# Two score blocks behind one product, and chain products two slots apart, in an attention kernel on one core

## The chip, the cores and the metric

The kernel runs on one core of a Trainium2 chip. The time is device microseconds (us) of one execution of the whole program. The engines are named as in the profile: PE (TensorE, matmuls), PEld (its weight loads, which run beside the matmuls), DVE (VectorE), ACT (ScalarE), POOL (GpSimd) and SP (SyncE, which here only issues DMAs). Each engine works through its own queue in order and waits on semaphores for the others.

## The reference

One layer of graph attention, for 128 graphs of 128 nodes, 768 features and 12 heads of 64, all in float32:

```python
h = jnp.maximum(_layernorm(x, axis=-1), 0.0)
q = _split_heads(h @ Wq + bq)          # likewise k, v
scores = jnp.einsum('bhqd,bhkd->bhqk', q, k) / jnp.sqrt(64)
scores = scores + beta * adj_e
scores = jnp.where(adj_e > 0, scores, -9e15)
probs = jax.nn.softmax(scores, axis=-1)
out = jnp.einsum('bhqk,bhkd->bhqd', probs, v)
x = x + out                            # heads put side by side again
```

## The kernel before

**Groups and slices.** Four graphs make a group; there are 32 groups, numbered 0 to 31. Of each group three matrix products are made, called slices: `qk0` (Q and K of the first six heads), `v` (V), and `qk1` (Q and K of the other heads). Group 0 is done in a plain way while the weights are prepared. From group 1 on each slice is a 3x3 block product done with a fast scheme of 15 block products instead of 27 (`PRODUCTS`, with sums of activations `SUMS_A` on one side and prepared weights on the other). One block product is again split into 7 zones, and is 14 matmuls in the program and 28 in the trace, where a float32 matmul stands twice (L547). The loop over the groups is written out in full; nothing is a loop on the chip.

**Slots.** The order of the 15 products in a slice is a table: `ZORDER` for `qk0` and `v`, `QORDER` for `qk1`, `LORDER` for the last group's `qk1`. A place in this order is called a slot, 0 to 14, and "slot 2 of V" is the third product of a V slice. All other work is hung on slots by hand with `then(slot, function, ...)`: it is put into the engines' queues after that slot's product and before the reading of its result, or, with `(slot, "post")`, after that reading. `later(f, n)` puts f off by n slots.

**Chains.** Each product belongs to one of four chains, a to d. A chain's products add up in one pair of PSUM banks, so the next product of a chain must wait until the running sum has been read. The reading goes to one or two of the six output blocks (r, j) of the slice: the first use of an output block copies it (in Q/K slices three instructions on ACT, L565 and L567 twice; in V slices first L561 on DVE and then L562 on ACT), and each later use adds on DVE (L571). There are four pairs of banks; chains, score blocks and the sums with V take and give them in turn (`take`, `give`).

**Homes and decoding.** An output block lies in one of eight tiles (`home`; one of them is a part of `sbig`). When its last product has been added, `decode` (L589 to L592, four instructions; in V slices L600 to L604) makes the final values in place, one slot later or as `LAG` says. It runs on POOL, except that in `qk1` the block that product 13 completes is decoded on DVE.

**Scores.** A score block (`scores`, L626) takes Q and K of one output column j for both r, 32 matmuls in the trace with 64 rows and 64 columns of the array (64\*64 in the profile), where products and the sums with V use 128 rows (128\*64). One slot later the mask is applied on DVE (L634), which also gives back the PSUM banks, and behind that the exponential on ACT (L636). Three blocks of `qk1` are placed in the next group's `qk0` slice, and the three of `qk0` in the group's own `v` slice. Weighing with V (L683), normalising (L654, L666), adding (L708) and storing follow at later slots.

**Other work on slots.** `norm` (L446) applies the layer norm of the next group on ACT, two instructions at a time; `to_hT` (L459) transposes on DVE; `sum_acts` (L464) makes the `SUMS_A` on DVE; `inner` (L469 to L471) adds on POOL; `row_stats` (L417 to L419) works on ACT out of a row loaded by DMA, for the group after the next. Prepared weights (`T`) are read from DRAM through a ring of 5 buffers (L335 by the loads of `T_qk` and `T_v`), one load being issued on SP after each product that used one; the products at the places listed in `RESIDENT` keep theirs in SBUF.

The order in which the engines get their instructions is exactly the order of these calls. The lines of the changed part in the kernel before:

```python
ZORDER = (1, 0, 3, 5, 2, 7, 10, 6, 11, 13, 4, 9, 14, 8, 12)
ORDER = {"qk0": ZORDER, "v": ZORDER, "qk1": QORDER}
RESIDENT = (3, 8, 12, 16, 20, 25, 29, 33, 35, 38, 41)
...
engine = nc.vector if sl == "qk1" and (n == 13 or last and n in (11, 12, 14)) else nc.gpsimd
...
then(3, scores, G - 1, 1, 2)          # qk0
then(5, scores, G - 1, 1, 0)
then((6, "post"), scores, G - 1, 1, 1)
...
then(0, scores, G, 0, 2)              # v
then(2, scores, G, 0, 1)
then(7, scores, G, 0, 0)
```

Of the kernel before, what the change touches and what calls it, by code (L numbers as in the profile page):

```python
# [108 lines left out]
ZORDER = (1, 0, 3, 5, 2, 7, 10, 6, 11, 13, 4, 9, 14, 8, 12)  # L109
QORDER = (4, 0, 1, 8, 2, 3, 5, 6, 7, 10, 9, 11, 13, 12, 14)  # L110
LORDER = (1, 4, 0, 8, 5, 2, 10, 3, 6, 7, 13, 9, 11, 12, 14)
ORDER = {"qk0": ZORDER, "v": ZORDER, "qk1": QORDER}
RING = 5
RESIDENT = (3, 8, 12, 16, 20, 25, 29, 33, 35, 38, 41)

# [10 lines left out]
def direct(ctx, tc, x, adj, wq, bq, wk, bk, wv, bv, beta, out, bad):  # L126
# [10 lines left out]
    nc = tc.nc  # L137
# [121 lines left out]

    sequence = [(sl, n) for sl in ("qk0", "v", "qk1") for n in ORDER[sl]]  # L260
    resident = {key: const.tile([P, 7, P], F32, name=f"res_{key[0]}_{key[1]}") for key in (sequence[at] for at in RESIDENT)}
# [59 lines left out]
        return steps  # L321

    def order_of(G, sl):
        return LORDER if G == NG - 1 and sl == "qk1" else ORDER[sl]

    ring = [(G, sl, n) for G in range(1, NG) for sl in ("qk0", "v", "qk1") for n in order_of(G, sl)
            if (sl, n) not in resident]
    nt = [0]

    def load_T():  # L330
        if nt[0] < len(ring):
            G, sl, n = ring[nt[0]]
            nt[0] += 1
            t = tz[G, sl, n] = work.tile([P, 7, P], F32, tag="T", name=f"T_{G}_{sl}_{n}", bufs=RING)
            nc.sync.dma_start(t, kept[sl, n])  # L335
# [125 lines left out]
    def sum_acts(G, name):  # L461
        _, a, b, sign = [row for row in SUMS_A if row[0] == name][0]
        t = full[G, name] = block(SPOT.index(name))
        nc.vector.tensor_tensor(t, full[G, a], full[G, b], ALU.add if sign > 0 else ALU.subtract)  # L464
# [33 lines left out]
    def later(f, slots=1):  # L498
        while len(deferred) < slots:
            deferred.append([])  # L500
        deferred[slots - 1].append(f)
# [6 lines left out]
    def turn():  # L508

        while between and next(between[0], None) is None:  # L510
            between.popleft()
# [4 lines left out]
    def home_qk(G, sl, r, j, zones=False):  # L516
        t = home_of[G, sl, r, j] = homes.popleft()
        return t if zones else t[:, 0:4].rearrange("p (i g) n -> p i (g n)", i=2)
# [12 lines left out]
    def product_z(G, sl, n):  # L531

        an, bn, chain, uses = PRODUCTS[n]
        mine = [i for i in order_of(G, sl) if PRODUCTS[i][2] == chain]
        first = n == mine[0]
        if first:
            banks[chain] = take()
        p = banks[chain].rearrange("p i (z w) -> p (i z) w", w=P)
        a = full[G, an]
        streamed = (sl, n) not in resident  # L540
        b = tz.pop((G, sl, n)) if streamed else resident[sl, n]
        for at, z in enumerate(ZONES):
            lhs, rhs = a[:, LEFT[z]], b[:, RIGHT[z]]
            if sl != "v":
                lhs, rhs = rhs, lhs
            for q in range(0, P, HD):
                nc.tensor.matmul(p[q:q + HD, at, :], lhs[:, q:q + HD], rhs, start=(first and at % 4 == 0),  # L547
                                 stop=True, skip_group_check=True)
            turn()
        if streamed:  # L550
            load_T()
        yield
        for (r, j), sign in uses:
            key = (G, sl, r, j)
            op = ALU.add if sign > 0 else ALU.subtract
            if key not in qk:
                left[key] = sum(k == (r, j) for q in PRODUCTS for k, _ in q[3])
                t = qk[key] = home_qk(*key, zones=True)
                if sl == "v":
                    bias = bv_b[:, j * 2 * P:(j + 1) * 2 * P].rearrange("p (i n) -> p i n", i=2)  # L560
                    nc.vector.tensor_tensor(t[:, 5:7], bias, p[:, 5:7], op)  # L561
                    nc.scalar.activation(t[:, 0:5], p[:, 0:5], AF.Copy, scale=float(sign))  # L562
                else:
                    oc = j + 3 * int(sl[2])
                    nc.scalar.activation(t[:, 0:5], p[:, 0:5], AF.Copy, scale=float(sign))  # L565
                    for at, of in ((5, 0), (6, 2)):
                        nc.scalar.activation(t[:, at], p[:, at], AF.Identity, bias=bqk[:, of, oc:oc + 1],  # L567
                                             scale=float(sign))
            else:
                t = qk[key]  # L570
                nc.vector.tensor_tensor(t, t, p[:, 0:7], op)  # L571
            left[key] -= 1
            if not left[key]:
                last = order_of(G, sl) is LORDER
                engine = nc.vector if sl == "qk1" and (n == 13 or last and n in (11, 12, 14)) else nc.gpsimd
                later(lambda r=r, j=j, engine=engine: decode(G, sl, r, j, engine), 1 if last else LAG.get((sl, n), 1))
        if n == mine[-1]:
            give(banks.pop(chain))
        yield
# [236 lines left out]
    def slice_z(G, sl, todo):  # L816
        run([product_z(G, sl, n) for n in order_of(G, sl)], todo)
# [163 lines left out]
    def then(at, f, *args):  # L981
        todo.setdefault(at, []).append(lambda: f(*args))

    def bias(G, *at):
        def go():
            if G not in steps:
                steps[G] = bias_steps(G)
            next(steps[G], None)
        for n in at:
            then(n, go)  # L990

    def attention(G, u, at, behind=5):
        for n, j in at:
            then(n - 3, load_xo, G, 3 * u + j)
            then((n, "post"), attend, G, 3 * u + j, behind)
# [6 lines left out]
    def turn_act(G, slots, behind=0):  # L1002
        for at, name in slots:
            then(at, to_hT, G, int(name[1]), int(name[2]))
            if behind is not None:
                then(at + behind, inner, G, name)

    def sums_at(G, slots):
        for at, name in slots:
            then(at, sum_acts, G, name)  # L1010
# [57 lines left out]
    for G in range(1, NG):  # L1068
        more = G + 1 < NG
        todo.clear()  # L1070
        then(3, scores, G - 1, 1, 2)
        then(5, scores, G - 1, 1, 0)
        then((6, "post"), scores, G - 1, 1, 1)
        attention(G - 1, 1, ((7, 2), (10, 0), (12, 1)))
        sums_at(G, ((0, "S7"), (1, "S0"), (4, "S5"), (7, "S14"), (9, "S11")))
        if G == 1:
            todo[0].insert(0, lambda: sum_acts(1, "S6"))
        if more:
            for g in range(2):
                for h in range(2):  # L1080
                    then((2 * g + h, "post"), norm, G + 1, g, 2 * h, 2 * h + 2)
            turn_act(G + 1, ((8, "A01"), (9, "A00"), (11, "A02")), None)
            then((12, "post"), load_x, G + 1, 1)
            if G + 2 < NG:
                then((7, "post"), row_stats, G + 2, 0)
                then((9, "post"), load_row, G + 2, 1)
        slice_z(G, "qk0", todo)

        todo.clear()
        then(0, scores, G, 0, 2)  # L1090
        then(2, scores, G, 0, 1)
        then(7, scores, G, 0, 0)
        if more:
            then((11, "post"), add_raw, G + 1)
            for n, at in enumerate((3, 4, 7, 8)):
                then((at, "post"), norm, G + 1, 2 + n // 2, n % 2 * 2, n % 2 * 2 + 2)
            turn_act(G + 1, ((10, "A11"),), 1)
            for at, name in ((4, "A01"), (5, "A00"), (6, "A02")):
                then(at, inner, G + 1, name)
            if G + 2 < NG:  # L1100
                for g, at in ((1, 1), (2, 5), (3, 10)):
                    then((at, "post"), row_stats, G + 2, g)
                    if g < 3:
                        then((at + 1, "post"), load_row, G + 2, g + 1)
        slice_z(G, "v", todo)

        todo.clear()
        if not more:
            break
        attention(G, 0, ((3, 2), (9, 1)))  # L1110
        attention(G, 0, ((12, 0),), 6)
        turn_act(G + 1, ((1, "A10"), (4, "A12")), 1)
        sums_at(G + 1, ((6, "S1"), (7, "S9"), (8, "S2"), (11, "S6"), (13, "S10")))
        bias(G + 1, 0, 2, 4)
        if G + 2 < NG:
            then(5, row_moments, G + 2, 6, 9)
            then((6, "post"), load_x, G + 2, 0)
        if G + 3 < NG:
            then((10, "post"), load_row, G + 3, 0)
        slice_z(G, "qk1", todo)  # L1120
# [158 lines left out]
```

## Time and profile before

| | |
|---|---|
| median of 3 runs | 2707.47 us (2703.18 to 2716.2) |
| profiled execution | 2712.82 us, its span 2711.0 us |
| PE busy | 2674.2 us, 99% of the span |
| PEld busy | 2568.3 us, 95% |
| DVE busy | 2188.4 us, 81% |
| POOL busy | 2096.0 us, 77% |
| ACT busy | 1762.5 us, 65% |
| DMA | 721.73 MB, mean 266 GB/s; the data queue's packets fill 86.4% of the 16 engines' time |

The profile is of one execution; its own time lies 0.2% above the median of the runs. A row of the timeline gives the start in us from the span's start, the length in us, engine, line of the kernel, operation, output tile and input tiles, shape and number of equal instructions in a row; in brackets stands the idle time before and what ended it. Matmuls overlap each other in the array, so the length of a group of matmuls reaches into the next; the pace of PE is read from the differences of the starts. A row of waits gives who waited for whom, then the us in total, the number of times, and the longest.

### The profile page before, as it was taken

The numbers are of one execution on the slowest core, as the hardware profiler recorded it, in microseconds if no ns is written. First come the engines' busy times: TensorE is split into PE (matmuls) and PEld (weight loads), VectorE is DVE, ScalarE is ACT, GpSimd is POOL, SyncE is SP. The second block draws the span as 40 slices with busy tenths as digits, with TensorE's granted clock in tenths as the row PEclk, the third lists the DMA queues.
The fourth block names the chain that finished last, engine by engine and source line by source line (L and its number), as shares of the span: only waits on it lengthen the run. The fifth ranks groups of instructions, "written<-read, shape, count | busy, mean of one in ns | idle before, by whom it ended". The sixth has DMA issues, their size and how long they took to land.

```text
span 2711.0 us, 121562 instructions
## 1 busy us (share of the span) xinstructions
PE 2674.2 (99%) x52029; PEld 2568.3 (95%) x52029; DVE 2188.4 (81%) x2705; ACT 1762.5 (65%) x4612; POOL 2096.0 (77%) x3034
## 2 busy tenths in 40 slices
PE   8999999999999999999999999999999999999997
PEld 7799999999999999999999999999999999999997
DVE  6878888788888788888788878788887888877885
ACT  2476666677666677666767666776666776667653
POOL 4867878777878877888778787778787778887783
PEclk9999999999999999999999999999999999999999
DMA  8789889899889898889899889898898988888875
GB/s 229 262 260 278 274 271 274 259 281 276 271 264 281 260 287 272 271 278 277 259 277 276 275 274 268 269 273 269 270 283 260 280 272 269 280 269 256 253 235 158
DMA packets 530342, 721.73 MB, mean 266 GB/s; under 512 B 105980, under 2 KB 374024, under 8 KB 529800
## 3 DMA queue, kind: packets, MB, share of 16 engines
q1 hardware_dynamic: 528640, 713.12, 86.4%
q8 instruction: 412, 6.75, 1.0%
q10 hardware_dynamic: 1160, 0.79, 0.1%
q14 instruction: 130, 1.06, 0.1%
HBM read 647.73 MB, written 66.05 MB: 263 GB/s over the span
## 4 chain that ended last, share of the span: by engine, by line
PE 87%; POOL 4%; DVE 3%; ACT 2%; DMA 1%; issue 1%; POOLq 0%; DVEq 0%; ACTq 0%
PE pair L547 74%; PE pair L626 7%; PE pair L683 6%; DMA sbig<-in_x_dram 1%; DVE home L571 1%; POOL home L590 1%; POOL home L589 1%; POOL home L592 1%; ACT sbig L419 0%; POOL home L591 0%; ACT sbig L417 0%; ACT home L562 0%; DVE e L634 0%; DVE prep_v L304 0%; ACT e L636 0%
## 5 line engine op out<-in xcount | busy, mean ns | idle before, releaser
L571 DVE TENSOR_TENSOR home<-home,pair 128x896 f32<-128x896 f32 x810 | 860.2, 1075 | 234.2 <-PE pair L547 130.4
L547 PE MATMUL pair<-sbig,T_qk 128*64 128x128 f32 x13888 | 888.6, 274 | 4.1 <-ACT e L666 3.1
L547 PEld LDWEIGHTS pair<-sbig,T_qk 128*64 128x64 f32 x13888 | 758.0, 137 | 17.8 <-issue 8.0
L666 ACT ACTIVATE e<-e,sm 128x64 f32<-128x64 f32 x1512 | 382.2, 341 | 123.5 <-DVE sm L654 123.2
L547 PE MATMUL pair<-A,T_qk 128*64 128x128 f32 x6076 | 415.1, 273 | 0.0
L547 PE MATMUL pair<-T_v,sbig 128*64 128x128 f32 x6944 | 414.2, 274 | 0.3 <-ACT home L562 0.3
L589 POOL TENSOR_TENSOR home<-home 128x256 f32<-128x256 f32 x297 | 227.2, 765 | 237.0 <-DVE home L571 237.0
L683 PE MATMUL pair<-v,e 128*64 128x65 f32 x6048 | 401.8, 221 | 0.0
L565 ACT ACTIVATE home<-pair 128x640 f32<-128x640 f32 x325 | 229.2, 705 | 261.5 <-PE pair L547 196.8
L547 PEld LDWEIGHTS pair<-T_v,sbig 128*64 128x64 f32 x6944 | 385.4, 137 | 6.3 <-issue 4.3
L683 PEld LDWEIGHTS pair<-v,e 128*64 128x64 f32 x6048 | 359.5, 137 | 3.6 <-DVE e L634 0.3
L547 PEld LDWEIGHTS pair<-A,T_qk 128*64 128x64 f32 x6076 | 331.7, 137 | 5.5 <-issue 5.5
L634 DVE SCALAR_TENSOR_TENSOR e<-pair,biasT 128x1024 f32<-128x1024 f32 x189 | 230.4, 1219 | 82.1 <-PE pair L626 82.0
L592 POOL TENSOR_TENSOR home<-home 128x256 f32<-128x256 f32 x297 | 276.3, 930 | 23.3
L590 POOL TENSOR_TENSOR home<-home 128x256 f32<-128x256 f32 x297 | 250.1, 842 | 23.3
L636 ACT ACTIVATE e<-e 128x1024 f32<-128x1024 f32 x189 | 200.2, 1059 | 64.7 <-DVE e L634 56.7
L446 ACT ACTIVATE x<-x,block 128x192 f32<-128x192 f32 x480 | 231.7, 540 | 0.0
L692 ACT ACTIVATE sm<-pair,tiny 128x8 f32<-128x8 f32 x189 | 49.3, 261 | 261.6 <-PE pair L683 261.6
L591 POOL TENSOR_TENSOR home<-home 128x128 f32<-128x128 f32 x297 | 196.9, 663 | 23.3
L547 PE MATMUL pair<-sbig,res_qk 128*64 128x128 f32 x3472 | 211.9, 273 | 0.0
L567 ACT ACTIVATE home<-pair,bqk 128x128 f32<-128x128 f32 x650 | 203.6, 374 | 0.0
L626 PE MATMUL pair<-home 64*64 64x128 f32 x5312 | 196.2, 277 | 6.3 <-issue 4.8
(192 smaller groups left out, 4699.9 us busy)
## 6 DMA issues: line engine op xcount, KB each, us to landing
T_qk<-kept_qk SPq DMA_DIRECT2D x713, 448.0 KB, 4.8
T_v<-kept_v SPq DMA_DIRECT2D x341, 448.0 KB, 4.9
xo<-in_x_dram SPq DMA_DIRECT2D x189, 256.0 KB, 4.5
out_dram<-xo SPq DMA_DIRECT2D x189, 256.0 KB, 5.9
x<-in_x_dram SPq DMA_DIRECT2D x248, 192.0 KB, 6.6
sbig<-in_x_dram SPq DMA_DIRECT2D x116, 384.0 KB, 6.5
kept_qk<-prep_qk SPq DMA_DIRECT2D x23, 448.0 KB, 2.9
adj<-in_adj_dram SPq DMA_DIRECT2D x128, 64.0 KB, 3.9
```

The lines of the kernel that those rows point to most:

```text
L446: nc.scalar.activation(t, t, AF.Relu, bias=shift[G, n], scale=rstd[G, n])
L547: nc.tensor.matmul(p[q:q + HD, at, :], lhs[:, q:q + HD], rhs, start=(first and at % 4 == 0), stop=True, skip_group_check=True)
L565: nc.scalar.activation(t[:, 0:5], p[:, 0:5], AF.Copy, scale=float(sign))
L567: nc.scalar.activation(t[:, at], p[:, at], AF.Identity, bias=bqk[:, of, oc:oc + 1], scale=float(sign))
L571: nc.vector.tensor_tensor(t, t, p[:, 0:7], op)
L589: e.tensor_tensor(t[:, 1:4:2], t[:, 1:4:2], twice(5), ALU.add)
L590: e.tensor_tensor(t[:, 2:5:2], t[:, 2:5:2], twice(1), ALU.add)
L592: e.tensor_tensor(t[:, 0:7:6], t[:, 0:7:6], twice(2), ALU.add)
L626: nc.tensor.matmul(ps[k:k + HD, i, g * N:(g + 1) * N], keys[r, k:k + HD], queries[r], start=True, stop=True)
L634: nc.vector.scalar_tensor_tensor(e, ps, SCORE_CAP * ISCALE, bias, op0=ALU.min, op1=ALU.add)
L666: nc.scalar.activation(o[:, r, b, 0:HD], pa[:, r, b, 0:HD], AF.Copy, scale=t[:, 1, r, b:b + 1])
L683: nc.tensor.matmul(pa[q:q + HD, 2 * g + i, :], k[:, q:q + HD], vt[G, "v", r, h // 4][:, 4 * g + h % 4, :], start=True, stop=True, skip_gro ...
```

## The change

In `qk0` of groups 2 to 31 and in `v` of all groups from 1 on, the products stand in a new order (`PORDER`), in which the third product belongs to the chain of the first, the fourth to the chain of the second, and chain b begins at slot 4 in place of slot 2 with its second product at slot 6. In both slices two score blocks now stand next to each other behind the third product (slot 2); they stood at slots 3 and 5 in `qk0` and at slots 0 and 2 in `v`. Group 1's `qk0` keeps the old order and the old places. In `qk1` the block that product 12 completes is decoded on DVE and the one of product 13 on POOL (it was the other way round; the last group decodes the same four on DVE as before). The sums S5 and S14 are made one slot later in `qk0`. The four calls of `norm` in `qk0` move from behind slots 0, 1, 2, 3 to behind slots 1, 2, 4, 5, and two of the four in `v` from 7 and 8 to 6 and 7. Since `RESIDENT` lists places in the order, other products' weights stay in SBUF, at the same slots as before.

```diff
+PORDER = (1, 0, 5, 2, 3, 10, 7, 6, 13, 11, 4, 9, 14, 8, 12)
-ORDER = {"qk0": ZORDER, "v": ZORDER, "qk1": QORDER}
+ORDER = {"qk0": PORDER, "v": PORDER, "qk1": QORDER}
...
     def order_of(G, sl):
+        if G == 1 and sl == "qk0":
+            return ZORDER
         return LORDER if G == NG - 1 and sl == "qk1" else ORDER[sl]
...
-                engine = nc.vector if sl == "qk1" and (n == 13 or last and n in (11, 12, 14)) else nc.gpsimd
+                engine = nc.vector if sl == "qk1" and (n == 12 or last and n in (11, 13, 14)) else nc.gpsimd
...
-        then(3, scores, G - 1, 1, 2)
-        then(5, scores, G - 1, 1, 0)
+        then(2 + (G == 1), scores, G - 1, 1, 2)
+        then(2 + 3 * (G == 1), scores, G - 1, 1, 0)
         then((6, "post"), scores, G - 1, 1, 1)
         attention(G - 1, 1, ((7, 2), (10, 0), (12, 1)))
-        sums_at(G, ((0, "S7"), (1, "S0"), (4, "S5"), (7, "S14"), (9, "S11")))
+        sums_at(G, ((0, "S7"), (1, "S0"), (5, "S5"), (8, "S14"), (9, "S11")))
...
-            for g in range(2):
-                for h in range(2):
-                    then((2 * g + h, "post"), norm, G + 1, g, 2 * h, 2 * h + 2)
+            for n, at in enumerate((1, 2, 4, 5)):
+                then((at, "post"), norm, G + 1, n // 2, n % 2 * 2, n % 2 * 2 + 2)
...
-        then(0, scores, G, 0, 2)
+        then(2, scores, G, 0, 2)
         then(2, scores, G, 0, 1)
         then(7, scores, G, 0, 0)
         if more:
             then((11, "post"), add_raw, G + 1)
-            for n, at in enumerate((3, 4, 7, 8)):
+            for n, at in enumerate((3, 4, 6, 7)):
                 then((at, "post"), norm, G + 1, 2 + n // 2, n % 2 * 2, n % 2 * 2 + 2)
```

## The prediction, made before the changed kernel had run

> **What bounds the kernel.** I read the page's busy times and its chain that ended last, then the windows of whole groups, then the timeline of PE, then those of the engines that PE waits for.
>
> ```profile
> PE 2674.2 (99%) x52029; PEld 2568.3 (95%) x52029; DVE 2188.4 (81%) x2705; ACT 1762.5 (65%) x4612; POOL 2096.0 (77%) x3034
> ...
> PE 87%; POOL 4%; DVE 3%; ACT 2%; DMA 1%; issue 1%; POOLq 0%; DVEq 0%; ACTq 0%
> ```
>
> ```profile
> 1037.68:1119.40 81.72, 81.71 (x1648) 79.40 (x1646) 67.39 (x80) 55.78 (x146) 65.53 (x95) 1.00 0.91 275
> 1777.30:1860.80 83.50, 82.09 (x1648) 79.52 (x1646) 67.51 (x80) 55.78 (x146) 65.50 (x95) 1.00 0.88 268
> ```
>
> The columns after the window are its length, PE, PEld, DVE, ACT and POOL busy, granted clock, DMA share, GB/s. A good group (number 12, first row) is PE from end to end at full clock. So time can come only from a faster pace of PE, or from its few waits (the second row, group 21, has 1.4 us of them). Everything else must only stay ahead of PE.
>
> The pace, around the start of V in group 12, and two products far from any score block:
>
> ```profile
> 1008.90 1.70 PE L547 MATMUL pair<-T_v,A 128*64 128x128 f32 x28
> 1010.43 1.70 PE L547 MATMUL pair<-res_v,A 128*64 128x128 f32 x28
> ...
> 1067.21 1.70 PE L547 MATMUL pair<-T_v,sbig 128*64 128x128 f32 x28
> 1068.84 0.67 PE L626 MATMUL pair<-sbig 64*64 64x128 f32 x16
> 1069.32 0.62 PE L626 MATMUL pair<-home 64*64 64x128 f32 x16
> 1069.87 1.75 PE L547 MATMUL pair<-res_v,sbig 128*64 128x128 f32 x28
> 1071.45 1.70 PE L547 MATMUL pair<-T_v,sbig 128*64 128x128 f32 x28
> ```
>
> ```profile
> 1069.21 0.29 PE L626 MATMUL pair<-sbig 64*64 64x128 f32 x4
> ```
>
> A product takes 1.53 us (1010.43 - 1008.90). The two products around this score block take 1071.45 - 1067.21 = 4.24 us, so the block costs 4.24 - 2 x 1.53 = 1.18 us. Inside it the pace is 0.11 us for 4 matmuls (1069.21 to 1069.32), 0.88 us for 32. The other 0.30 us lies at the two edges, where 128\*64 and 64\*64 matmuls meet. The lookup of line L626 says the same of the entry (idle time before its instructions, and how often):
>
> ```profile
>   issue: 44.4, 184
>   POOL home L592: 8.5, 27
> ```
>
> 0.24 us of idle before a block (44.4/184), which no semaphore explains.
>
> **The change, part by part.**
>
> *Blocks side by side.* Two blocks one after the other have two edges in place of four. That is once in `qk0` of groups 2 to 31 (30) and once in each V slice of groups 1 to 31 (31): 61 x 0.30 = 18.3 us less. No row shows two blocks side by side, so the bounds are 0 (each block pays its edges whatever stands beside it) and 0.30. I take 0.30, since inside a block the pace changes between tiles of different homes without any cost (1068.84 to 1069.87 crosses from `sbig` to `home`). The Trainium skill, "TensorEngine Tiling (Array Packing)", Key Properties, says that changing the tiling mode, not just the tile, drains TensorE; by that rule the upper bound holds, and the 0.30 us at the edges agrees.
>
> *The swapped decodes.* The block behind slot 6 of `qk0` nearly always waits in its last quarter:
>
> ```profile
> 1050.86 1.34 PE L626 MATMUL pair<-home 64*64 64x128 f32 x32
> 1052.13 1.75 PE L547 MATMUL pair<-A,T_qk 128*64 128x128 f32 x28
> ```
>
> ```profile
> 1037.23 0.79 POOL L592 TENSOR_TENSOR home<-home 128x256 f32<-128x256 f32 x1
> 1040.16 1.11 POOL L589 TENSOR_TENSOR sbig<-sbig 128x256 f32<-128x256 f32 x1 [2.15 <-DVE sbig L571]
> 1043.43 1.46 POOL L592 TENSOR_TENSOR sbig<-sbig 128x256 f32<-128x256 f32 x1
> ...
> 1050.97 0.72 POOL L592 TENSOR_TENSOR home<-home 128x256 f32<-128x256 f32 x1
> ```
>
> It takes 1.27 us (1052.13 - 1050.86) where the block above took 1.03 (1069.87 - 1068.84): 0.24 us, for POOL's decode that ends at 1051.69. POOL was idle 2.15 us before it began product 12's block at 1040.16. With product 13's block on POOL, whose last addition is one product older, it goes on at 1038.02, the next two decodes come some 2 us earlier, and this wait goes: 27 times (row above) x 0.24 = 6.5 us less. New users: the pair of blocks at slot 2 starts near 1037.68 + 3 x 1.53 + 0.1 = 1042.4 and needs the POOL block in its second half, 1042.9. The slowest decode shown took 4.73 us (1040.16 to 1044.89), which from 1038.02 would end at 1042.75: covered, barely. If POOL is 1 us later, 30 x 0.85 us come back. DVE's four instructions stay in number; they move one slot later.
>
> *Chain products two slots apart.* From one product's start to the start of the next but one are 3.06 us when no score block lies between: slots 0 to 2 in both slices, 4 to 6. Readings of today:
>
> ```profile
> 1039.48 0.70 ACT L565 ACTIVATE home<-pair 128x640 f32<-128x640 f32 x1 [2.36 <-issue]
> 1040.08 0.62 ACT L567 ACTIVATE home<-pair,bqk 128x128 f32<-128x128 f32 x2
> ...
> 1069.48 0.71 ACT L562 ACTIVATE home<-pair 128x640 f32<-128x640 f32 x1 [0.39 <-DVE home L561]
> ```
>
> ```profile
> 1073.27 1.09 DVE L571 TENSOR_TENSOR home<-home,pair 128x896 f32<-128x896 f32 x1 [0.17 <-PE pair L547]
> ```
>
> In `qk0` the reading of slot 0 ends at 1040.70; slot 2 would start at 1037.68 + 3.06 = 1040.74 (the group starts where its window does). In V it ends at 1070.19, against 1067.21 + 3.06 = 1070.27. On DVE (slots 4 to 6) the product at 1071.45 is read by 1074.36, 2.91 us. So all three fit by 0.04 to 0.15 us if their engine is free, and none has a reserve. I charge 0.02 us for each of the 61 slices, 1.2 us; the bounds are 0 and 0.2 (one semaphore late at each of the three places).
>
> *Engine queues ahead of these.* ACT: the norm behind slot 0 of `qk0` goes, which frees it before the reading of slot 1, needed at slot 3 after the two blocks; the moved norms keep their number and their reader, L459 from slot 8 on, lies far behind: 0. DVE in `qk0`:
>
> ```profile
> 1036.75 0.68 DVE L589 TENSOR_TENSOR home<-home 128x256 f32<-128x256 f32 x1
> ...
> 1038.66 0.42 DVE L592 TENSOR_TENSOR home<-home 128x256 f32<-128x256 f32 x1
> ...
> 1042.95 1.34 DVE L464 TENSOR_TENSOR sbig<-sbig 128x896 f32<-128x896 f32 x1
> 1044.22 1.07 DVE L571 TENSOR_TENSOR home<-home,pair 128x896 f32<-128x896 f32 x1
> ...
> 1046.05 1.21 DVE L634 SCALAR_TENSOR_TENSOR e<-pair,biasT 128x1024 f32<-128x1024 f32 x1
> ```
>
> It runs late here: sum S0 ends at 1044.29. Slot 2's reading moves to ACT, so the first mask follows at once and ends at 1045.5; chain b, at slot 4, takes that block's banks and starts near 1037.68 + 4 x 1.53 + 2.06 = 1045.9 (2.06 being two blocks, 2 x 0.88 + 0.30). Slack 0.4 us, cost 0, price below. The decode before it (first two rows, 2.3 us in all) stays in that queue, one slot later. S5 and S14 still come before their products. SP: every load, store and ring read keeps its slot, since the resident places are the same; in group 0 other prepared products are stored, in equal number: 0.
>
> *Row statistics in V.* In six groups PE waits at slots 9 and 10:
>
> ```profile
> 508.94 1.75 PE L547 MATMUL pair<-T_v,sbig 128*64 128x128 f32 x28 [0.34 <-ACT home L562]
> 511.19 1.75 PE L547 MATMUL pair<-res_v,A 128*64 128x128 f32 x28 [0.51 <-DVE e L634]
> ```
>
> ```profile
> 506.06 0.84 ACT L417 ACTIVATE sbig<-sbig 128x768 f32<-128x768 f32 x1 [1.73 <-DMA sbig<-in_x_dram]
> ...
> 508.20 0.68 ACT L562 ACTIVATE home<-pair 128x640 f32<-128x640 f32 x1
> ```
>
> ```profile
> PE pair L547 <- DVE e L634: 2.5, 6, 0.5
> ```
>
> ACT stands at `row_stats` (behind slot 5) for its DMA, and the reading of slot 6 (product 10) queues behind it; DVE's adding and the mask follow. In the new order product 10 is at slot 5, read ahead of the statistics: 6 x (2.25 - 1.53) = 4.3 us less; bounds 0 and 4.3.
>
> *Instructions for PE.* Some blocks at slot 2 of V stop in the middle:
>
> ```profile
> 1812.73 0.88 PE L626 MATMUL pair<-home 64*64 64x128 f32 x22
> 1814.99 0.59 PE L626 MATMUL pair<-home 64*64 64x128 f32 x10 [1.39 <-issue]
> 1815.52 3.28 PE L547 MATMUL pair<-T_v,sbig 128*64 128x128 f32 x56
> ```
>
> ```profile
> PE pair L626 <- issue: 6.5, 8, 1.9
> ```
>
> ```profile
> q8 instruction: 412, 6.75, 1.0%
> ```
>
> This block took 2.79 us for 1.03, 1.76 lost where 1.39 shows as idle; so the 8 stops cost about 6.5 + 8 x 0.37 = 9.5 us. The instruction queue moves 6.75 MB in 412 packets, 16.4 KB each, and I read the stop as PE having used up one packet before the next came. In the built program a group is 3327 PE instructions before and 3322 after. If a packet holds 256, the seam between packets moves by 1 or by 6 instructions from group to group: before it stays in this block all through, after it wanders over half a slice. But side by side blocks use instructions faster. I leave the 9.5 us as they are; bounds 0 and twice that. The Trainium skill, "Runtime: NRT & Kernel Launch", Instruction fetch mechanics, gives 256 instructions to a block and calls crossing it mostly hidden; the idle row above disagrees, and by the rule alone this part would be zero in both kernels.
>
> **Sum.** -18.3 - 6.5 - 4.3 + 1.2 = -27.9 us: 2712.8 becomes 2684.9. The median is 5.3 us below that execution, which gives 2679.6. I say 2682, between the two.
>
> **Rivals.** A difference within 0.5% (13.5 us) is about what a measurement of this kernel can't tell from none; faster means below 2694.
>
> - *DVE late in `qk0`* (slower). The bank for slot 4 comes from the first mask. If DVE reaches it more than 0.4 us later than reckoned, slot 4 and, two slots on, slot 6 wait in all 30 slices. DVE now decodes while POOL does too, and the rows above leave it next to no idle time. Were it late by a whole decode (2.3 us), 30 x 1.9 = 57 us come back: 2684.9 + 57 = 2742. It decides from about 1.8 us late (27.9 + 13.5 = 41.4 us over 30 slices, plus the slack). Against it: the decode stands in DVE's queue ahead of these already.
> - *Instructions run short.* One of four V slices stops today, at 1.2 us each. At one of two in all 61 double blocks it is 37 us for 9.5: 2684.9 + 27 = 2712, no change. For it: 64 matmuls in 2.06 us, against 3.1 for two products (56).
> - *The edges belong to the block.* Then 18.3 us stay: 2703, within 0.5%. Against it: the idle before the weight loads, with no wait named.
>
> **Chances.** Forecast 0.70, DVE late 0.08, instructions 0.12, edges 0.10. Faster: nearly all of the first and a third of the second, 0.74; same 0.16; slower 0.10. The forecast's own range is 2667 (stops gone as well) to 2694. The range for 8 in 10 takes in the edges' case and part of the instructions': 2666 to 2706.
>
> **What would show it.** Right: in V, score rows at slot 2 with 64 matmuls in about 2.06 us and one edge on each side; "issue" before L626 down to some 123 times; the block behind slot 6 of `qk0` in 1.03 us; no wait of L547 for L634 at slot 10. Wrong: a new wait of L547 for L634 (slot 4) or for L567, L562, L571 (slots 2 and 6); waits of L626 for L592 at slot 2; more idle by "issue" inside the blocks.

## The result, and the profile after

The changed kernel takes 2694.64 us (median of 8 runs, 2691.86 to 2699.36) where the kernel before, on the same chip, takes 2708.84 (8 runs): a ratio of 0.9946, 95% interval 0.9934 to 0.9958, or 14.2 us less. The forecast was 2682. The time lies inside the range for 8 in 10 and on the right side; it is just above the forecast's own range, which ended at 2694, and the gain is half of the 27.9 us that the sum gave. The profiled execution took 2692.31 us, its span is 2690.5; it stands 20.5 us below the profiled execution of before, which lay 4 us above its median.

The page of the changed kernel, engine times and the chain of work that ended last (L547 of before is now L550, L626 is L629, L634 is L637, L464 is L467, L571 is L574, L589 to L592 are L592 to L595):

```profile
PE 2650.9 (99%) x52029; PEld 2564.3 (95%) x52029; DVE 2185.2 (81%) x2705; ACT 1751.2 (65%) x4612; POOL 2111.8 (78%) x3034
...
PE 77%; DVE 13%; DMA 3%; issue 2%; POOL 1%; ACT 0%; SPq 0%; POOLq 0%; DVEq 0%; ACTq 0%
```

DVE's share of the chain was 3% and is 13%, though its busy time is the same to 0.2%. It limits the time in some stretch now. To find which, the timeline of PE, first in V (group 12), then in `qk0` of the same group:

```profile
1062.59 1.72 PE L550 MATMUL pair<-T_v,sbig 128*64 128x128 f32 x28
1064.24 0.67 PE L629 MATMUL pair<-sbig 64*64 64x128 f32 x16
1064.73 1.49 PE L629 MATMUL pair<-home 64*64 64x128 f32 x48
1066.15 3.28 PE L550 MATMUL pair<-T_v,sbig 128*64 128x128 f32 x56
1069.26 1.70 PE L550 MATMUL pair<-res_v,sbig 128*64 128x128 f32 x28
```

```profile
1034.75 1.10 PE L629 MATMUL pair<-home 64*64 64x128 f32 x32
...
1036.66 1.75 PE L550 MATMUL pair<-sbig,res_qk 128*64 128x128 f32 x28
1038.68 4.81 PE L550 MATMUL pair<-sbig,T_qk 128*64 128x128 f32 x84 [0.28 <-DVE e L637]
1043.42 1.10 PE L629 MATMUL pair<-home 64*64 64x128 f32 x32
1044.45 1.75 PE L550 MATMUL pair<-A,T_qk 128*64 128x128 f32 x28
```

In V three products and two blocks take 1069.26 - 1062.59 = 6.67 us; less 3 x 1.53 this leaves 2.08 us for the two blocks, where two blocks apart cost 2 x 1.18 = 2.36: 0.28 us less. The pair in `qk0` takes the same 1.91 us from its first matmul to the product behind it (1066.15 - 1064.24; 1036.66 - 1034.75), but begins 0.03 us later behind its slot (median over the slices), so that it saves 0.25 us. The block behind slot 6 now takes 1.03 us (1044.45 - 1043.42) in place of 1.27. These were the gains hoped for. What is new is the wait at 1038.68. Slot 3 began at 1036.66, and a product behind a block takes 1.58 us, so slot 4 could have begun at 1038.24; it began 0.44 us late.

The list of waits of the same kernel shows how often:

```profile
PEld pair L550 <- DVE e L637: 14.7, 29, 0.7
PE pair L550 <- DVE e L637: 7.3, 25, 0.3
...
PE pair L550 <- issue: 2.8, 5, 1.4
...
PE pair L550 <- DMA T_qk<-kept_qk: 2.4, 5, 0.9
PE pair L550 <- DMA T_v<-kept_v: 2.2, 2, 1.8
...
PE pair L629 <- issue: 2.0, 2, 1.4
```

25 times 0.44 us are 11.0 us given back; the starts of slots 3 and 4 give 12.0 us over all 30 slices, against 1.58 us for each. The idle time in PE's row (7.3 us) is smaller than that, and that of the weight loads ahead of the products (first row, 14.7 us) larger.

The chain of work of this kernel, around that wait (start, length, what):

```profile
1022.79 0.24 PE pair L550 x4
...
1023.05 1.09 DVE home L574
...
1025.59 1.95 DVE home L574 x2
1027.54 1.10 DVE sbig L467
...
1030.85 0.77 DVE sbig L592
...
1034.88 1.95 DVE sbig L467 x2
...
1037.42 1.22 DVE e L637
```

From 1023.05 to 1038.64 every link is DVE's, apart from short pieces of "issue" in which DVE's timeline shows no idle time either: it reads products, makes the sums S6 and S10, adds an attention result (L711), decodes (L592 to L595), reads once more (L574), makes the sums S7 and S0 (L467 twice) and only then reaches the mask (L637) for whose banks slot 4 waits. DVE has no reserve from slot 10 of `qk1` on. Inside that stretch one piece has grown. DVE and POOL of the changed kernel at that time:

```profile
1030.77 0.83 DVE L592 TENSOR_TENSOR sbig<-sbig 128x256 f32<-128x256 f32 x1
1031.64 0.83 DVE L593 TENSOR_TENSOR sbig<-sbig 128x256 f32<-128x256 f32 x1
1032.51 0.43 DVE L594 TENSOR_TENSOR sbig<-sbig 128x128 f32<-128x128 f32 x1
1032.97 0.91 DVE L595 TENSOR_TENSOR sbig<-sbig 128x256 f32<-128x256 f32 x1
1033.80 1.07 DVE L574 TENSOR_TENSOR home<-home,pair 128x896 f32<-128x896 f32 x1
```

```profile
1030.15 1.17 POOL L592 TENSOR_TENSOR home<-home 128x256 f32<-128x256 f32 x1
1031.40 0.79 POOL L593 TENSOR_TENSOR home<-home 128x256 f32<-128x256 f32 x1
...
1032.87 0.72 POOL L595 TENSOR_TENSOR home<-home 128x256 f32<-128x256 f32 x1
```

DVE's decode takes 3.1 us (1030.77 to 1033.88) where it took 2.3. Before, it ran from 1036.75 to 1039.08; the prediction shows its first and last step (0.68 and 0.42 us), and these are the two between:

```profile
1037.46 0.83 DVE L590 TENSOR_TENSOR home<-home 128x256 f32<-128x256 f32 x1
1038.34 0.29 DVE L591 TENSOR_TENSOR home<-home 128x128 f32<-128x128 f32 x1
```

POOL was idle from 1038.02 to 1040.16 (the prediction's rows), so DVE's last two steps ran with POOL idle, and the first two for the most part beside it. The four steps have grown by 0.15, 0, 0.14 and 0.49 us: most of it in the last two. The exchange of decodes has filled that idle time: now the two engines decode side by side all through, and DVE's steps go in time with POOL's.

The readings of the row statistics in V no longer stop PE. Where PE waited twice (508.94 and 511.19, slots 9 and 10 of group 5's V), the timeline of after has the products of these slots at 503.01 and 504.54, and two products in 3.06 us (506.07 - 503.01):

```profile
503.01 1.70 PE L550 MATMUL pair<-T_v,A 128*64 128x128 f32 x28
504.54 1.70 PE L550 MATMUL pair<-res_v,A 128*64 128x128 f32 x28
506.07 3.23 PE L550 MATMUL pair<-T_v,sbig 128*64 128x128 f32 x56
```

### The profile page after: what moved, and what is told of

It reads as the page before. It is cut to its first block, busy times and chain, and to the rows that moved or that the text cites. A ratio compares the mean times of both kernels' runs of the same rounds, so it can differ in the third digit from the quotient of the medians.

```text
span 2690.5 us, 121410 instructions
## 1 busy us (share of the span) xinstructions
PE 2650.9 (99%) x52029; PEld 2564.3 (95%) x52029; DVE 2185.2 (81%) x2705; ACT 1751.2 (65%) x4612; POOL 2111.8 (78%) x3034
## 4 chain that ended last, share of the span: by engine, by line
PE 77%; DVE 13%; DMA 3%; issue 2%; POOL 1%; ACT 0%; SPq 0%; POOLq 0%; DVEq 0%; ACTq 0%
PE pair L550 67%; PE pair L686 5%; PE pair L629 5%; DVE home L574 4%; DVE sbig L467 3%; DVE e L637 1%; DMA T_qk<-kept_qk 1%; DMA T_v<-kept_v 1%; DMA out_dram<-xo 1%; DVE xo L711 1%; DVE home L595 1%; DVE home L593 1%; DVE home L592 1%; DVE sbig L574 0%; DVE home L594 0%
## 5 line engine op out<-in xcount | busy, mean ns | idle before, releaser
L574 DVE TENSOR_TENSOR home<-home,pair 128x896 f32<-128x896 f32 x810 | 860.9, 1076 | 276.0 <-PE pair L550 236.9
L550 PE MATMUL pair<-sbig,T_qk 128*64 128x128 f32 x13020 | 827.8, 273 | 9.7 <-DVE e L637 7.3
L550 PEld LDWEIGHTS pair<-sbig,T_qk 128*64 128x64 f32 x13020 | 708.0, 137 | 20.9 <-DVE e L637 14.0
L550 PE MATMUL pair<-A,T_qk 128*64 128x128 f32 x6944 | 463.7, 273 | 0.0
L592 POOL TENSOR_TENSOR home<-home 128x256 f32<-128x256 f32 x297 | 265.8, 895 | 226.2 <-DVE home L574 222.2
L550 PE MATMUL pair<-T_v,sbig 128*64 128x128 f32 x6944 | 418.3, 274 | 5.5 <-issue 2.8
L550 PEld LDWEIGHTS pair<-T_v,sbig 128*64 128x64 f32 x6944 | 381.5, 137 | 20.1 <-issue 17.4
L550 PEld LDWEIGHTS pair<-A,T_qk 128*64 128x64 f32 x6944 | 378.1, 137 | 5.9 <-issue 5.5
L550 PE MATMUL pair<-sbig,res_qk 128*64 128x128 f32 x4340 | 288.5, 273 | 0.0
L595 POOL TENSOR_TENSOR home<-home 128x256 f32<-128x256 f32 x297 | 240.3, 809 | 23.3
L550 PEld LDWEIGHTS pair<-sbig,res_qk 128*64 128x64 f32 x4340 | 234.6, 137 | 5.3 <-issue 5.3
L594 POOL TENSOR_TENSOR home<-home 128x128 f32<-128x128 f32 x297 | 213.9, 720 | 23.3
L637 DVE SCALAR_TENSOR_TENSOR e<-pair,biasT 128x1024 f32<-128x1024 f32 x189 | 225.0, 1216 | 3.2 <-PE pair L629 3.2
L639 ACT ACTIVATE e<-e 128x1024 f32<-128x1024 f32 x189 | 193.7, 1065 | 47.0 <-DVE e L637 39.1
L472 POOL TENSOR_TENSOR A<-A 128x256 f32<-128x256 f32 x186 | 169.9, 914 | 59.2 <-DVE A L462 59.2
```

The costliest lines, as they stand in the source:

```text
L592: e.tensor_tensor(t[:, 1:4:2], t[:, 1:4:2], twice(5), ALU.add)
L594: e.tensor_tensor(t[:, 4], t[:, 4], t[:, 6], ALU.add)
L595: e.tensor_tensor(t[:, 0:7:6], t[:, 0:7:6], twice(2), ALU.add)
L637: nc.vector.scalar_tensor_tensor(e, ps, SCORE_CAP * ISCALE, bias, op0=ALU.min, op1=ALU.add)
L639: trailing.append(lambda: nc.scalar.activation(e, e, AF.Exp, scale=1.0 / ISCALE))
```

## Experiments

The theory: the V part gains what was forecast, and the `qk0` part loses its own gain because DVE, slowed beside POOL and without reserve, brings the first mask late. The rivals: it is only a matter of the order on DVE in `qk0`; or the pairs themselves are worth less.

**S0 later.** The sum S0 stands ahead of the mask on DVE; here it is made at slot 3, behind the masks.

```diff
-        sums_at(G, ((0, "S7"), (1, "S0"), (5, "S5"), (8, "S14"), (9, "S11")))
+        sums_at(G, ((0, "S7"), (3, "S0"), (5, "S5"), (8, "S14"), (9, "S11")))
```

> The changed kernel with the sum S0 of the Q/K slice moved from slot 1 to slot 3, behind the two masks. Theory (DVE reaches the first mask too late, so the product at slot 4 waits 0.46 us for its banks, and 0.05 us more at the next edge, in 26 of 30 slices): the waits of L550 for L637 go from 25 to none or a few, about 12 us less than the changed kernel, 2683 us, ratio to the kernel before 0.990. A small new wait at slot 6 (up to 0.15 us, since the reading of slot 4 follows the moved sum on DVE) may take back 4 us of it. Rival (the mask is late because the score blocks or the homes are late, not because of DVE's queue): no difference to the changed kernel, ratio 0.9946.

Measured: 2693.0 us, ratio 0.9948 (0.9929 to 0.9967), as the whole change; the gain that the theory expected did not come. The wait of slot 4 for the mask is gone from this kernel's list of waits, and another has come:

```profile
PEld pair L550 <- DVE home L574: 7.2, 24, 0.3
```

Now the reading of slot 4's product, which stands behind S0, is late for slot 6. By the starts of the products, slot 3 has lost its 0.41 us (mean), and slots 4 to 6 together take 0.49 us more. Changing the order inside the stretch moves the wait and does not shorten it: DVE has too much to do there.

**The V part alone, and the `qk0` part alone.** First the kernel before with V's new order, pair and norms (the first two lines below, with V's lines of the change); then the changed kernel with V's order, places and norms as before (the last two).

```diff
-ORDER = {"qk0": ZORDER, "v": ZORDER, "qk1": QORDER}
+ORDER = {"qk0": ZORDER, "v": PORDER, "qk1": QORDER}
...
-ORDER = {"qk0": PORDER, "v": PORDER, "qk1": QORDER}
+ORDER = {"qk0": PORDER, "v": ZORDER, "qk1": QORDER}
```

> Only the V slices are changed; the Q/K slices, the decodes and their norms stay as in the kernel before. Theory (each pair of blocks saves two edges, 0.28 us in V, 31 times, and the reading of product 10 ahead of the row statistics saves 4.3 us): 8.8 + 4.3 = 13 us less than before, ratio 0.995, and the waits at the last quarter of the block behind slot 6 of the Q/K slice stay. Rival (the edges belong to the block, the gain of the changed kernel came from the swapped decodes): 4 us less, ratio 0.9985. Stops at seams between instruction packets may move either by 5 us.

> Only the Q/K slices (order, places of the score blocks, sums, norms, decodes) are changed; the V slices stay as in the kernel before. Theory: 30 x 0.26 = 7.7 us from the edges and 6.5 us from the wait behind slot 6 are gained, 13.2 us are lost to the mask that slot 4 waits for: 1 us less than before, ratio 0.9996, with some 25 waits of L550 for L637. Rival (the Q/K part carries the gain, for instance by the swapped decodes alone): 10 us less or more, ratio 0.996.

V alone: 2689.47 us, ratio 0.9933 (0.9921 to 0.9945). `qk0` alone: 2706.59 us, ratio 0.9995 (0.9986 to 1.0005). So the V part makes the whole gain and the `qk0` part, with its three edits, makes nothing, as expected. V alone gains 16 to 18 us in its two runs, where 13 were expected. In its first profile the 31 V slices take 18.4 us less than before: 8.7 by the pair, 5.4 at slots 8 to 14, most of it where PE waited behind the row statistics, and 4.2 at slots 1 to 4, where the stops lie that the rows put down to issue; these differ from one execution to the next. In the list of waits of `qk0` alone the wait for the mask stands as in the whole change (27 of the 32, with 9.0 us, are at slot 4; the other five are V's waits of before at slot 10):

```profile
PE pair L550 <- DVE e L637: 10.9, 32, 0.5
```

To compare V alone with the whole change without a difference of chips, both ran again side by side.

> The V part alone once more, on the same chip as the whole change. Theory (the first Q/K part's three edits cancel to nothing, or cost a little beside V's): ratio to the kernel before 0.9933, and below the whole change by 3 to 5 us. Rival (the two runs differed only by the chip): the two are the same to within 2 us.

> The whole change once more, beside the V part alone on the same chip. Theory: ratio to the kernel before 0.9946, above the V part alone by 3 to 5 us. Rival: the same as the V part alone to within 2 us.

V alone 2688.35 us, ratio 0.9946 (0.9928 to 0.9964); the whole change 2692.91 us, ratio 0.9957 (0.9943 to 0.9971). V alone is 4.6 us lower here too, at the size expected, but the two intervals overlap: that the `qk0` part costs something is likely, that it gains nothing is shown by its own run.

**V's pair taken apart.** The whole change with V's first block back at slot 0; all else as in the change.

```diff
-        then(2, scores, G, 0, 2)
+        then(0, scores, G, 0, 2)
         then(2, scores, G, 0, 1)
```

> The changed kernel with the first of V's two blocks put back to slot 0, so that the two stand apart again while the order of the products stays new. Theory (the edges between the two kinds of matmul cost 0.28 us for each pair, whatever else stands there): 31 x 0.28 = 8.8 us more than the changed kernel, about 2703 us, ratio 0.998. Rival (the block costs what it costs wherever it stands): no difference to the changed kernel, ratio 0.9946.

Measured: 2700.02 us, ratio 0.9971 (0.9962 to 0.9981): 0.25% or 6.8 us above the whole change (0.9946), where 8.8 were expected. By the starts in its trace the two blocks cost 2.36 us again (median), 0.28 more than side by side. The edges are a price of the meeting of blocks and products, not of the block.

**The decodes back.** The whole change, but product 12 decoded on POOL and 13 on DVE.

```diff
-                engine = nc.vector if sl == "qk1" and (n == 12 or last and n in (11, 13, 14)) else nc.gpsimd
+                engine = nc.vector if sl == "qk1" and (n == 13 or last and n in (11, 12, 14)) else nc.gpsimd
```

> The changed kernel with products 12 and 13 decoded by the engines that decoded them before (12 on GpSimd, 13 on VectorE). Theory: the second block of the pair at slot 2 waits for GpSimd's decode, by about 1.4 us in each of 30 slices, less the 13 us of the wait for the mask that goes: about 28 us more than the changed kernel, 2722 us, ratio 1.005; VectorE's decode falls back to about 2.3 us. Rival (which engine decodes does not matter, VectorE is short anyway): as the changed kernel, 0.9946.

Measured: 2717.23 us, ratio 1.0041 (1.0029 to 1.0054), 26 us above the whole change, about as expected (28): the pair at slot 2 needs the exchange. Its timeline of PE shows the second block waiting in the middle for POOL's last decode step:

```profile
1042.29 0.45 PE L629 MATMUL pair<-sbig 64*64 64x128 f32 x8 [1.08 <-POOL sbig L595]
```

And DVE's decode is fast again (2.3 us), and with it the first mask is early enough:

```profile
1041.58 1.21 DVE L637 SCALAR_TENSOR_TENSOR e<-pair,biasT 128x1024 f32<-128x1024 f32 x1
```

It ends 7.67 us into the slice (median of the 30), in the whole change 8.63; slot 4 could start 8.2 us into it (1038.24 - 1030.01, see below). So with the fast decode slot 4 would not have waited even if the pair had not been late, and in this list of waits no product waits for a mask at slot 4. The groups of DVE instructions of groups 2 to 31, first of the whole change, then of this kernel (total, then ns of one):

```profile
L595 DVE TENSOR_TENSOR home<-home 128x256 f32<-128x256 f32 x24 | 21.8, 907 | 0.8
```

```profile
L595 DVE TENSOR_TENSOR home<-home 128x256 f32<-128x256 f32 x24 | 10.2, 425 | 0.8
```

The same instruction on the same shape takes 907 ns when POOL decodes beside it and 425 ns when POOL stands idle.

**The exchange without the pair.** V alone, and with it the exchange of decodes; `qk0` keeps its old order.

```diff
-                engine = nc.vector if sl == "qk1" and (n == 13 or last and n in (11, 12, 14)) else nc.gpsimd
+                engine = nc.vector if sl == "qk1" and (n == 12 or last and n in (11, 13, 14)) else nc.gpsimd
```

> The V part alone, and with it the exchange of the decodes of products 12 and 13 between VectorE and GpSimd, in the old order of the first Q/K slice. Theory: the block behind slot 6 stops waiting for GpSimd's decode (6.5 us of excess in the kernel before), and VectorE's queue, without the pair's earlier needs, has the time for its slower decode: 6.5 us less than the V part alone, about 2683 us, ratio 0.991. Rival: VectorE's decode beside GpSimd's, 3.1 us in place of 2.3 us, delays the mask by as much as the exchange saves: as the V part alone, 0.9933.

Measured: 2705.9 us, ratio 1.0002 (0.9992 to 1.0012). Both expectations missed; the exchange by itself costs all that the V part gains, 15 to 19 us (0.9933 and 0.9946 against 1.0002). The waits that the exchange was to remove, of V alone, and what stands in their place with the exchange:

```profile
PEld pair L629 <- POOL home L595: 6.3, 27, 1.5
```

```profile
PE pair L629 <- DVE e L637: 12.9, 30, 0.5
```

The block behind slot 6 no longer waits for POOL; it waits longer, in all 30 slices, for the mask that gives it its banks:

```profile
1041.66 1.75 PE L550 MATMUL pair<-sbig,T_qk 128*64 128x128 f32 x28
1043.85 1.10 PE L629 MATMUL pair<-home 64*64 64x128 f32 x32 [0.44 <-DVE e L637]
1044.89 1.75 PE L550 MATMUL pair<-A,T_qk 128*64 128x128 f32 x28
```

The two rows of waits give 6.6 us more. The starts of the products give more: slots 5 and 6, each with its block, take 12.2 us more over the 30 slices than in V alone (slot 6 3.21 us for 2.87 in the mean), which is most of the 15 us between the two profiled executions. DVE's decode takes 3.1 us here too, and S0 ends 7.51 us into the slice for 6.54 in V alone (medians). So the late mask shows in the old order as well, without the pair.

**S1 earlier.** If DVE is short of time over a stretch, work must be pulled ahead of it. In the whole change DVE is idle for 0.74 us at 1013.86, just before slot 6's reading and S1:

```profile
1014.60 1.09 DVE L574 TENSOR_TENSOR home<-home,pair 128x896 f32<-128x896 f32 x1 [0.74 <-PE pair L550]
```

```diff
-        sums_at(G + 1, ((6, "S1"), (7, "S9"), (8, "S2"), (11, "S6"), (13, "S10")))
+        sums_at(G + 1, ((5, "S1"), (7, "S9"), (8, "S2"), (11, "S6"), (13, "S10")))
```

> The changed kernel with the S1 step moved from slot 6 to slot 5 of the second Q/K slice, into the 0.74 us for which VectorE waits idle just before S1 in the profile after (the row at 1014.60). Theory (VectorE falls short of its queue by about 0.46 us between S1 and the first mask, and work pulled into idle time ahead of the stretch fills the gap): most of the wait of slot 4's product for the mask goes, up to 13 us less than the changed kernel, about 2683 us, ratio to the kernel before 0.9905. Rival (it is only another order, and the wait moves, as it did with S0 at slot 3): same as the changed kernel, 0.9946.

Measured: 2695.75 us, ratio 0.9964 (0.9953 to 0.9975). No gain; the wait for the mask is still there (11.2 us, 27 times). The timeline of DVE of this kernel says why:

```profile
1020.86 1.09 DVE L574 TENSOR_TENSOR home<-home,pair 128x896 f32<-128x896 f32 x1 [0.79 <-PE pair L550]
```

The idle time has only moved to slot 10's reading, which cannot start before PE has made the product. So the stretch begins here and not at S1; this is also where the chain of the whole change passes from PE to DVE (1022.79 to 1023.05).

**S6 earlier as well.** S6, the sum behind slot 11, goes to slot 10, into that 0.79 us.

```diff
-        sums_at(G + 1, ((6, "S1"), (7, "S9"), (8, "S2"), (11, "S6"), (13, "S10")))
+        sums_at(G + 1, ((5, "S1"), (7, "S9"), (8, "S2"), (10, "S6"), (13, "S10")))
```

> The changed kernel with S1 at slot 5 (as in the run before with S1 alone, which left VectorE idle for 0.79 us at slot 10 of the second Q/K slice and still made slot 4 of the first wait for the mask) and with S6 moved from slot 11 to slot 10, into that idle time. Theory (the stretch in which VectorE is short begins with the reading behind slot 10: in the chain of the profile after, every step from 1023.05 to the mask at 1037.42 is VectorE's): about 0.7 us less VectorE work in the stretch, so the 0.46 us wait of slot 4's product goes in nearly all slices: some 12 us below the run with S1 alone, about 2684 us, ratio to the kernel before 0.992. Rival (VectorE's lateness is set by the order within the first Q/K slice, or the later reading behind slot 10 stops TensorE by as much): as with S1 alone, 0.9964, or above it.

Measured: 2681.81 us, ratio 0.9918 (0.9898 to 0.9938), beside the whole change at 2692.91 on the same chip: 11 us less, against 11 to 12 reckoned from the waits. Its wait list has two waits for the mask in place of 25, and its page's chain and the start of slot 4 (1.62 us behind slot 3) show PE as the only limit again:

```profile
PE 92%; DVE 2%; POOL 1%; DMA 1%; issue 1%; ACT 0%; SPq 0%; DVEq 0%; POOLq 0%; ACTq 0%
```

```profile
PE pair L550 <- DVE e L637: 0.4, 2, 0.2
```

```profile
1029.82 1.75 PE L550 MATMUL pair<-sbig,res_qk 128*64 128x128 f32 x28
1031.44 2.83 PE L550 MATMUL pair<-sbig,T_qk 128*64 128x128 f32 x47
```

This kernel is faster than the whole change (the intervals lie apart). Its median is 6.5 us below V alone on the same chip, but those two intervals touch (0.9938 and 0.9928), so that is likely and not shown. DVE's decode still runs beside POOL's in it, at the same length; what it has is the reserve to bear it.

**The seam between instruction packets.** The kernel before, with 16 small matmuls after the warm-up, 64 more PE instructions (each matmul is two, with a weight load each). They only add work.

```diff
+    for n in range(16):
+        nc.tensor.matmul(warm[:, 1, 0:1], ident, ident[:, 0:1], start=True, stop=True)
```

> The kernel before with 16 one-column matmuls added after the warm-up, which shifts every later TensorE instruction by 64 places (each runs as four). Theory (the stops that the rows put down to issue come at every 256th instruction of TensorE): the eight stops leave the score block at slot 2 of V and stand 64 instructions earlier in the work, in the products of about slot 2; the total stays within 10 us of the kernel before, with 2 us at most for the added matmuls. Rival (the stops belong to the score block or to what it depends on): they stay in the score block of slot 2.

Measured: 2708.15 us, ratio 1.0003 (0.9993 to 1.0013). The row that put 6.5 us of idle in score blocks (L626) down to issue is gone from the list of waits; one for products has come, and the timeline shows such a stop:

```profile
PE pair L547 <- issue: 2.4, 5, 1.5
```

```profile
578.05 0.82 PE L547 MATMUL pair<-T_v,sbig 128*64 128x128 f32 x11
580.37 1.15 PE L547 MATMUL pair<-T_v,sbig 128*64 128x128 f32 x17 [1.51 <-issue]
581.45 1.10 PE L626 MATMUL pair<-home 64*64 64x128 f32 x32
```

It stands behind 11 of the 28 matmuls of the slot-2 product in group 6. In the kernel before, a stop stood behind 22 of the 32 matmuls of the block in group 21 (1814.99). Between the two places lie 17 + 22 = 39 matmuls, 78 instructions with their weight loads; 15 groups later the seam stands 15 instructions further on (3327 to a group, one less than 13 x 256), which leaves 63 for the 64 added. The traces bear out the step of 256: counting all of PE's instructions from the start, every stop of 0.15 us or more that the rows between 215 and 2600 us put down to issue, 14 in these two profiles and 81 in the other eleven, stands at place 193, 194 or 195 of a stretch of 256. The stops belong to every 256th instruction of PE, whatever stands there; most of these places show none.

## Why the prediction was right, and where it failed

*Blocks side by side, -18.3.* Right, a little too large: 0.28 us for each pair in V and 0.25 in `qk0`, for 0.30 forecast; 31 x 0.28 + 30 x 0.25 = 16.2. That the edges belong to the block (a rival at 0.10) falls with V's pair taken apart.

*The swapped decodes, -6.5.* The wait went as forecast (1.03 us for the block behind slot 6; 7.3 us over the 30 slices by the starts, a stop in group 9 left out), but the step counted DVE's four instructions at their old duration. POOL's rows in the prediction show the 2.15 us of idle time in which DVE made the second half of its decode; that the exchange would fill them was written down as POOL's gain and not as DVE's cost.

*Chain products two slots apart, +1.2.* Right within what can be seen: slot 2 of neither slice has a wait of its product for a copy on ACT that comes again from group to group. Slot 2 of `qk0` starts more than 0.1 us late in groups 2, 5 and 6 alone, 1.8 us in all, and there the rows of PE name the weights' DMA.

*DVE in `qk0`: "Slack 0.4 us, cost 0".* This is the step that failed. The reckoning took S0 to end 6.61 us into the slice (1044.29 - 1037.68) as before. It ended at 1037.42 in a slice that began at 1036.66 - 3 x 1.53 - 2.06 = 1030.01, so 7.41 us into it: 0.80 us later, and 0.78 is what the decode grew by. The slack of 0.4 us is used up and 0.44 us lost, 25 times. With the decode fast (products 12 and 13 decoded as before) the mask ended 0.96 us earlier in the slice, in time for slot 4. The rival "DVE late in `qk0`" named the mechanism, and even that DVE decodes while POOL does too; it was weighed only by the point from which it turns the sign, and the sum took nothing for the part of it below that point.

*Row statistics, -4.3.* Right; the waits at slots 9 and 10 of V are gone, 4.4 us in the six groups by the starts.

*Instructions for PE, unchanged.* Right in size: stops that showed 6.5 us of idle in eight score blocks now show 4.8 us in seven places, five of them products, since the seam wanders. The waits for loads of weights (2.4 and 2.2 us, in the list of waits above) are new: neither profile with the old order has one, and each with the new order in `qk0` or V has some, 1.5 to 4.6 us. So they probably come of the change; through what, no run tells.

The sum with the measured terms: -16.2 - 7.3 - 4.4 + 12.0 = -15.9, between the 14.2 us of the medians and the 20.5 of the two profiled executions. By the starts in these two profiles the 30 `qk0` slices together are 0.7 us shorter and the 31 V slices 16.1; the other 3.7 lie outside these slices, nearly all of it ahead of group 1's V. That the time fell inside the range was in part luck: the range reached to 2706 for the case that the edges stay and for more stops, and what took the time up there was the wait for the mask, which had no part in the sum.

## What to carry to other kernels

Before work is moved into an engine's idle time, look at what runs on the neighbouring engine in just that time, and price it at the duration it has when both work. A wait behind an engine that has no idle time over a long stretch is not cured by another order within the stretch: follow the chain back to where it passes from the other engine, and pull work ahead of that place. A rival that names a mechanism has a price below its turning point too, and that price belongs into the sum.

## What the runs showed of the hardware

DVE and POOL slow each other on some instructions. DVE's 128x256 addition inside SBUF takes 425 ns with POOL idle and 907 ns beside POOL's decode. Between 200 and 2600 us of the whole change's profile, a sum of two SBUF tiles (L467, 128x896) takes 1.08 us with POOL idle and 1.37 us in the mean where POOL works all through it. The addition of a PSUM tile of the same size (L574) takes 1.09 and 1.08 us in these two cases (1.07 at 1033.80). The Trainium skill, "SBUF — State Buffer", section "SBUF: two separate sides", says that a DVE instruction with two inputs in SBUF needs a port pair that it shares with GpSimd, as a lock held for the whole instruction. The rows agree, in that DVE's steps start in turn with POOL's and only those with both inputs in SBUF grow; the runs don't separate a lock from another kind of sharing.

PE stops for up to 1.9 us at places 256 instructions apart, in an unrolled kernel whose data queue fills 86% of the DMA engines' time. In the kernel before it did so, for 0.15 us or more, at nine of some 400 such places. Shifting the whole program by 64 instructions moved the stops and left the time as it was. That the next packet of instructions is not there yet is the likely reason; no run delayed or hastened a packet.
